# Attention in a four-layer network: products of values and probabilities in four column tiles, row sums on VectorE

## The chip, the cores and the metric

The kernel runs on one core of a Trainium2 chip. The metric is the time on the device in microseconds (us), as the median of several runs. Everything is computed in fp32.

## What is computed

The input x is a batch of B = 4 images with 384 channels and 64 x 64 positions. Four layers follow one another, each of the form x + layer(groupnorm(x)). The change lies in the first layer, whose core is single-head attention over the N = 4096 positions of an image:

```python
# layer 0, p = 96 of the 384 channels, per image
y   = layernorm_over_channels(groupnorm(x)[:, :96])
qkv = batchnorm(w_qkv @ y)               # 16 + 16 + 96 rows
q, k, v = qkv[:16], qkv[16:32], qkv[32:]
a   = softmax(q.T @ k * 0.25, axis=-1)   # 4096 x 4096
o   = v @ a.T                            # 96 x 4096
out = batchnorm(w_proj @ relu(concat([o, rest_of_channels])))
```

For each query position the 4096 exponentials are summed, and the weighted sum of the 96 value rows is divided by that sum. The second layer is a gated convolution layer with an 8 x 8 Fourier filter; layers three and four are convolutions and small products that the change does not touch.

## The kernel before, in words

The first phase, `phase_a`, covers layer 0 and most of layer 1. The attention of an image (`attention`) has 8 blocks `i` of 512 queries; each block has 8 steps `c` of 512 keys, so there are 64 steps an image and 256 in all. A step does the following.

- `scores` (line 715): four products with a contraction over 32 partitions, one for each of four groups `g` of 128 keys. They stand in four row tiles of the matrix array and fill a tile of four banks of PSUM (`sc_s`, one buffer).
- The exponentials (line 723): two ScalarE instructions of 128 x 1024 turn the scores into a tile `probs` of 128 keys by 4 x 512 (two buffers). The scores and exponentials of the next step are issued ahead of the products of this one, with raised priority.
- The products (line 752): four matmuls, each with all 128 keys of a group as the contraction, 128 columns of `vt` as the stationary operand, and 512 queries streaming. They add up over the 32 groups of a block in one PSUM bank `av` (tag "a", two buffers, so that successive blocks alternate).

`vt` has 128 columns: 96 value rows and 32 columns of ones, which the weight `wv` makes from the constant row of the normalised input. Rows 96 to 127 of `av` are thus 32 copies of the softmax sum. `finish` takes their reciprocal on VectorE (line 735) and scales and clips the 96 value rows in three instructions of 32 rows (line 738), since both operands lie 32 partitions wide. The result `xm` goes to the projection, `layer0_end` (lines 774 to 795), whose pieces are issued one a step during the next block.

What else runs beside the steps of image `b` is set by `side_by_side`: it takes pieces from `others`, which first reads the statistics of the next image (`x_norm`), then works through `layer1` of the image before, and makes `qkv` of the next image in between. Each piece carries a weight, and per step as many are issued as their even spread over 64 steps asks for. In `layer1` a tile of 16 columns goes through `t_m` (line 871), `coef_m` (886, emptied by VectorE at 888), `back_m` (896), and each band of eight rows through nine taps on VectorE for each of three channel blocks (line 948), which carry no weight, and then an output product `out_m` (965, 966; emptied by VectorE at 969). All these products, the projection's `proj_m` (785, emptied by VectorE at 792) and those of `qkv` share one PSUM tag, "m", with two buffers. PSUM has eight banks here: four for scores, two of tag "a", two of tag "m".

The order on each engine is fixed when the program is built: a scheduler keeps the order of issue as priority, lets an instruction go ahead where an earlier one isn't ready by its estimate, and puts in the semaphores. Every engine then works in that order.

Of the kernel before, what the change touches and what calls it, by code (L numbers as in the profile page):

```python
# [21 lines left out]
F32 = mybir.dt.float32  # L22
AF = mybir.ActivationFunctionType
ALU = mybir.AluOpType
# [5 lines left out]
P = 128  # L30
PD = 96
# [7 lines left out]
TAPS = (2, 2, 2, 2, 2, 2, 4, 4)  # L39

UNITS = C // 32

_CONST_COLS = {}
_VEC_COLS = {}
# [182 lines left out]
class _Builder:  # L227
    def __init__(self, ctx, tc, ins, out):
# [18 lines left out]

        self.tok = self.dram.tile([UNITS, B, 32, N], F32, tag="tok", name="tok")

# [137 lines left out]
    def qkv_weights(self, pool):  # L387

        nc = self.nc
        w = self.wk("wq_raw", "lx", 2)[:, 0:PD]
        nc.scalar.dma_start(w, self.ins["w_qkv"])
        inv, shift = self.bn_scale_shift(
            "bn1", self.vec("bn1_m"), self.vec("bn1_v"), self.vec("bn1_g"), self.vec("bn1_b")
        )
        nc.vector.tensor_scalar(w, w, inv, None, ALU.mult)
        pt = self.pm("wq_pt")
        nc.tensor.transpose(pt[0:PD, 0:P], w, self.ident)
        wt = self.wk("wq_t", "ln", 3)[0 : PD + 1, 0:P]  # L400
        raw = self.wk("wq_rawt", "lx", 2)[0:PD, 0:P]
        nc.vector.tensor_copy(raw, pt[0:PD, 0:P])
        nc.vector.tensor_scalar(wt[0:PD, :], raw, self.vec("ln_w", PD), None, ALU.mult)
        pb = self.pm("wq_pb")
        nc.tensor.matmul(pb[0:1, 0:P], lhsT=self.vec("ln_b", PD), rhs=raw, start=True, stop=False)
        nc.tensor.matmul(pb[0:1, 0:P], lhsT=shift, rhs=self.ident, start=False, stop=True)
        nc.scalar.copy(wt[PD : PD + 1, :], pb[0:1, 0:P])

        self.wq4 = pool.tile([PD + 1, 4, 32], F32, tag="wq4", name="wq4")
        self.wk4 = pool.tile([PD + 1, 4, 32], F32, tag="wk4", name="wk4")  # L410
        self.wv = pool.tile([PD + 1, P], F32, tag="wv", name="wv")
        for t in (self.wq4, self.wk4, self.wv):
            nc.gpsimd.memset(t, 0.0)
        nc.gpsimd.memset(self.wk4[PD : PD + 1, :, 0:1], 1.0)
        nc.gpsimd.memset(self.wv[PD : PD + 1, PD:], 1.0)
        for g in range(4):
            nc.vector.tensor_copy(self.wq4[:, g, 1:17], wt[:, 0:16])
            nc.vector.tensor_copy(self.wk4[:, g, 1:17], wt[:, 16:32])
        nc.vector.tensor_copy(self.wv[:, 0:PD], wt[:, 32:P])
        self.score_bound(pool, wt)  # L420

    def score_bound(self, pool, wt):
# [183 lines left out]
    def qkv_tiles(self):  # L606


        q = [None] * 8
        k4 = self.big.tile([P, 8, P], F32, tag="k4", name="k4", bufs=2)  # L610
        vt = self.big.tile([P, 32, P], F32, tag="vt", name="vt", bufs=2)
        return q, k4, vt

    def qkv(self, b, q, k4, vt):
        nc = self.nc

        xc, xn = [None] * 8, [None] * 8
        xc[0] = self.centered(b, 0)
        yield 1.0
        xn[0] = self.layer_norm(xc[0])  # L620
        xc[1] = self.centered(b, 1)
        yield 2.0
        for i in range(8):
            if i + 2 < 8:
                xc[i + 2] = self.centered(b, i + 2)
                yield 1.0
            if i + 1 < 8:
                xn[i + 1] = self.layer_norm(xc[i + 1])
                yield 1.0
# [12 lines left out]
            m = self.pm("v_m")  # L642
            mv = m.rearrange("p (c d) -> p c d", d=P)
            for c in range(4):
                nc.tensor.matmul(mv[:, c, :], lhsT=xa[:, c * P : (c + 1) * P], rhs=self.wv, start=True, stop=True)
            nc.vector.tensor_copy(vt[:, 4 * i : 4 * i + 4, :], mv)
            yield 2.8
# [55 lines left out]
    def attention(self, b, q, k4, vt):  # L703
# [3 lines left out]
        tc, nc = self.tc, self.nc  # L707
# [20 lines left out]
                )  # L728
            return p

        def finish(av):

            xm = self.work.tile([P, NJ, 512], F32, tag="xm", name="xm", bufs=1)
            rd = self.wk("av_rd", "rd", 1)
            nc.vector.reciprocal(rd[PD:P], av[PD:P])
            for g in range(3):
                at = slice(32 * g, 32 * g + 32)
                nc.vector.scalar_tensor_tensor(xm[at, 0], av[at], 0.0, rd[PD:P], ALU.max, ALU.mult)  # L738
            return xm

        st = self.stats_tile("xa_st")
        steps = [(i, c) for i in range(8) for c in range(8)]
        ahead = scores(*steps[0])
        done, end = None, iter(())
        for n_step, (i, c) in enumerate(steps):
            p = ahead
            if n_step + 1 < len(steps):
                ahead = scores(*steps[n_step + 1])
            if c == 0:
                av = self.pa("av")  # L750
            for v in range(4):
                nc.tensor.matmul(  # L752
                    av,
                    lhsT=vt[:, 4 * c + v, :],
                    rhs=p[:, v * 512 : (v + 1) * 512],
                    start=c == 0 and v == 0,
                    stop=c == 7 and v == 3,
                )
            next(end, None)
            if c == 1 and done is not None:  # L760
                end = self.layer0_end(b, i - 1, finish(done), st)
            if c == 7:
                done = av
            yield
        for _ in self.layer0_end(b, 7, finish(done), st):
            pass
        self.norm1 = self.norm_of_stats(st)

# [217 lines left out]
    def phase_b(self):  # L986
# [5 lines left out]
        with ExitStack() as ctx:  # L992
# [17 lines left out]
            self.units(cp)  # L1010
            self.unit_x = [[] for _ in range(UNITS)]
            for u in range(UNITS):
                st = self.bt_p.tile([P, 2, 16, 6], F32, tag="st", name="st")
                strips = self.unit_strips(u + 1) if u + 1 < UNITS else iter(())
                tok = self.unit_tok(u - 1) if u else self.unit_strips(0)
# [8 lines left out]
                self.conv_norms(u, st)  # L1024
            for _ in self.unit_tok(UNITS - 1):
                pass
# [859 lines left out]
```

## Time and profile before

| | |
|---|---|
| median of 3 runs | 4973.22 us (4967.2 to 4978.35) |
| span of the profiled execution | 4964.9 us |
| time around the span | not listed apart; the median lies 8.3 us above the span |
| TensorE busy | 4552.7 us (92%) |
| VectorE busy | 2769.8 us (56%) |
| ScalarE busy | 2136.4 us (43%) |
| attention: first to last product, line 752 | 81 to 2253 us of the span |

In a row of the page's slices each digit is the busy share of one fortieth of the span, in tenths. In a row of a group, the text after the line number names engine, operation, what is written from what, sizes and count; then come the busy time, the mean of one instruction in ns, and the idle time of the engine just before, with what ended it. A matmul of fp32 operands leaves two records in the profile, one for each of its two passes, and as many weight loads (PEld). Ends of matmuls are modelled; the distance from one start to the next is the better measure. In a row of the timeline the first two numbers are start and duration in us; neighbouring instructions of one line are merged.

### The profile page before, as it was taken

To read this page: it belongs to the slowest core of one execution; us is meant where nothing else is said; L and a number is where in the kernel's file an instruction comes from. 1 tells how busy PE (TensorE), PEld (TensorE's weight loads), DVE (VectorE), ACT (ScalarE), POOL (GpSimd) and SP (SyncE) were. 2 spreads that over 40 slices of the span, in tenths; PEclk is the share of its full clock that TensorE was granted. 3 is DMA by queue.
4 is the path that set the end of the run, shared out by engine and by line. 5 is a ranking of instruction groups with operands and counts; after the bars stand their busy time and mean duration, and the time that the engine had idled before them with its cause. 6 is when DMAs were issued, how large, how long until landed. Compare 5 with 4: busy or idle time off the path is not lost.

```text
span 4964.9 us, 47732 instructions
## 1 busy us (share of the span) xinstructions
PE 4552.7 (92%) x17665; PEld 2564.5 (52%) x17665; DVE 2769.8 (56%) x4438; ACT 2136.4 (43%) x2873; POOL 777.5 (16%) x593
## 2 busy tenths in 40 slices
PE   5999999999999999998989999699999998677988
PEld 2343444434443344444557888444444443577888
DVE  5322465644666445555867778655531112667898
ACT  4444344454444444444435666411123333764321
POOL 1000000000000000000025555100000001125554
PEclk9999999999999999998989999799999999699999
DMA  5210211211111111112338999776664443896776
GB/s 169 73 47 30 85 54 55 72 56 39 64 64 51 55 45 58 58 57 78 120 122 276 291 292 292 250 278 256 256 245 157 153 152 132 316 343 203 239 255 227
DMA packets 346710, 752.64 MB, mean 152 GB/s; under 512 B 22779, under 2 KB 173158, under 8 KB 337510
## 3 DMA queue, kind: packets, MB, share of 16 engines
q1 hardware_dynamic: 280728, 475.46, 30.1%
q0 software_dynamic: 32640, 151.28, 7.9%
q10 hardware_dynamic: 33102, 122.77, 6.3%
q8 instruction: 143, 2.34, 0.2%
q14 instruction: 97, 0.79, 0.0%
HBM read 447.16 MB, written 302.25 MB: 151 GB/s over the span
## 4 chain that ended last, share of the span: by engine, by line
PE 45%; DVE 9%; DMA 4%; ACT 3%; issue 3%; POOL 1%; SPq 0%; ACTq 0%; DVEq 0%; POOLq 0%
PE h_s L1380 10%; PE h_m L1432 10%; PE conv_m L1156 9%; PE av L752 3%; PE t_m L871 2%; PE conv_m L1757 2%; DVE acc L948 2%; DMA wmix<-in_mix_t 1%; DMA g_h<-h 1%; PE out_m L966 1%; PE proj_m L785 1%; PE sc_s L715 1%; DVE toep L1744 1%; PE taps_m L941 1%; DVE toep L1137 1%
## 5 line engine op out<-in xcount | busy, mean ns | idle before, releaser
L752 PE MATMUL av<-probs,vt 128*128 128x512 f32 x2048 | 965.6, 607 | 0.0
L723 ACT ACTIVATE probs<-sc_s 128x1024 f32<-128x1024 f32 x512 | 500.9, 1021 | 789.8 <-PE av L752 783.7
L752 PEld LDWEIGHTS av<-probs,vt 128*128 128x128 f32 x2048 | 371.7, 192 | 468.1 <-issue 461.0
L1156 PE MATMUL conv_m<-toep,z 128*128 128x256 f32 x2304 | 519.4, 385 | 10.6 <-DVE toep L1137 5.1
L948 DVE SCALAR_TENSOR_TENSOR acc<-band,vecs,acc 128x512 f32<-128x512 f32 x708 | 496.9, 747 | 45.7 <-POOL band L909 39.9
L1432 PE MATMUL h_m<-f_h,cm_w_t 128*128 128x512 f32 x1152 | 496.7, 595 | 8.7 <-ACT f_h L1422 8.7
L1156 PEld LDWEIGHTS conv_m<-toep,z 128*128 128x128 f32 x2304 | 439.4, 193 | 71.0 <-DVE z L1089 4.9
L1757 PE MATMUL conv_m<-toep,z 128*128 128x128 f32 x3072 | 392.8, 286 | 42.1 <-DVE toep L1744 19.2
L1757 PEld LDWEIGHTS conv_m<-toep,z 128*128 128x128 f32 x3072 | 378.7, 202 | 44.4 <-POOL toep L1744 18.2
L1380 PE MATMUL h_s<-e_tok,cm_w_t 128*128 128x512 f32 x768 | 363.4, 596 | 5.5 <-DVE e_tok L1365 5.5
L1137 POOL TENSOR_TENSOR toep<-w,band 128x1536 f32<-128x1536 f32 x94 | 324.0, 3447 | 278.0 <-PE conv_m L1156 232.0
L1432 PEld LDWEIGHTS h_m<-f_h,cm_w_t 128*128 128x128 f32 x1152 | 220.0, 191 | 285.4 <-issue 273.3
L715 PE MATMUL sc_s<-q,k 32*128 32x512 f32 x2048 | 296.3, 647 | 21.9 <-ACT probs L723 21.4
L1440 DVE BATCH_NORM_STATS2 h_st<-f_h 128x6 f32<-128x512 f32 x96 | 66.4, 694 | 429.1 <-ACT f_h L1439 429.1
L871 PE MATMUL t_m<-w_in_t,xb 128*128 128x384 f32 x768 | 276.7, 495 | 3.4 <-DVE coef L888 2.1
L1387 ACT COPY e_h<-h_s 128x1024 f32<-128x1024 f32 x96 | 97.2, 1012 | 401.5 <-PE h_s L1380 401.5
L785 PE MATMUL proj_m<-xm,w_proj_t 128*128 128x512 f32 x576 | 265.2, 599 | 4.6 <-DVE xm L738 3.5
L792 DVE SCALAR_TENSOR_TENSOR x_res<-proj_m,bn_c,x_res 128x512 f32<-128x512 f32 x96 | 71.8, 748 | 319.0 <-PE proj_m L785 315.9
L1380 PEld LDWEIGHTS h_s<-e_tok,cm_w_t 128*128 128x128 f32 x768 | 147.0, 192 | 189.5 <-issue 183.2
L1389 DVE BATCH_NORM_STATS2 h_st<-e_h 128x6 f32<-128x512 f32 x192 | 123.4, 685 | 202.8 <-ACT e_h L1387 202.8
L871 PEld LDWEIGHTS t_m<-w_in_t,xb 128*128 128x128 f32 x768 | 142.9, 192 | 139.0 <-issue 59.3
L1380 PE MATMUL h_s<-z,cm_w_t 128*128 128x512 f32 x384 | 196.2, 593 | 0.0
(380 smaller groups left out, 6206.2 us busy)
## 6 DMA issues: line engine op xcount, KB each, us to landing
d<-d_o ACTq DMA_DIRECT2D x96, 512.0 KB
c_d<-d SPq DMA_DIRECT2D x96, 512.0 KB
hid<-e_h ACTq DMA_DIRECT2D x16, 3072.0 KB
f_h<-hid SPq DMA_DIRECT2D x16, 3072.0 KB
x_in<-in_x SPq DMA_DIRECT2D x96, 256.0 KB
x_res<-in_x SPq DMA_DIRECT2D x32, 768.0 KB
xa<-x_res POOLq DMA_DIRECT2D x32, 768.0 KB, 3.9
xa_in<-xa SPq DMA_DIRECT2D x32, 768.0 KB
```

What stands on the lines that cost most here:

```text
L715: nc.tensor.matmul(s[:, g], lhsT=k4[32 * g : 32 * g + 32, c], rhs=q[i][32 * g : 32 * g + 32], start=True, stop=True,)
L723: nc.scalar.activation(p[:, h * 1024 : (h + 1) * 1024], s[:, 2 * h : 2 * h + 2].rearrange("p a b -> p (a b)"), AF.Exp, scale=0.25,)
L752: nc.tensor.matmul(av, lhsT=vt[:, 4 * c + v, :], rhs=p[:, v * 512 : (v + 1) * 512], start=c == 0 and v == 0, stop=c == 7 and v == 3,)
L785: nc.tensor.matmul(m, lhsT=self.w_proj[:, j, o * P : (o + 1) * P], rhs=xm[:, j], start=j == 0, stop=j == NJ - 1,)
L871: nc.tensor.matmul(m[:, 0:C], lhsT=xb[:, j], rhs=self.w_in[:, j, :], start=j == 0, stop=j == NJ - 1,)
L948: nc.vector.scalar_tensor_tensor(out, src(j, k), w, done, ALU.mult, ALU.add)
L1137: eng.tensor_tensor(t, self.w53[:, at : at + 192].rearrange("p (m n) -> p m n", n=8).unsqueeze(2).to_broadcast([P, 24, 8, 8]), band.rearra ...
L1156: nc.tensor.matmul(m[:, c * 256 : (c + 1) * 256], lhsT=self.z_[:, at : at + P], rhs=t[:, 12 * c + 4 * i : 12 * c + 4 * i + 4].rearrange("p ...
L1380: nc.tensor.matmul(s[:, v, :], lhsT=w1[:, j, o * P : (o + 1) * P], rhs=t[j][:, v * 512 : (v + 1) * 512], start=j == 0, stop=j == NJ - 1,)
L1389: nc.vector.bn_stats(st[:, o, 8 * b + 2 * i + v, :], h[:, o, v * 512 : (v + 1) * 512])
L1432: nc.tensor.matmul(m, lhsT=w2[:, o, j * P : (j + 1) * P], rhs=h[:, o, v * 512 : (v + 1) * 512], start=o == 0, stop=o == 5,)
L1757: nc.tensor.matmul(m[:, ch * P : (ch + 1) * P], lhsT=self.z_[:, at : at + P], rhs=t[:, 8 * c + 2 * i : 8 * c + 2 * i + 2].rearrange("p m a ...
```

## The change

The columns of ones go: `wv` and `vt` are 96 wide. The products of a step become twelve matmuls in place of four: for each of the four key groups `v`, the 96 value rows are taken as three slices `s` of 32. Each such matmul writes 32 partitions, one column tile `g` of the array. The table `PLAN` deals them out: three rounds of four, in which each column tile has one matmul. As twelve jobs of three slices don't divide into four tiles by slice, there are two banks, `av[0]` and `av[1]`, both of tag "a"; slice 0 is summed in tiles 0 and 3 of the first bank, slice 1 in tile 1 of the first and tile 0 of the second, slice 2 in tile 2 of the first and tile 1 of the second.

The softmax sums are made apart. In each step VectorE adds the two halves of `probs` (128 x 1024 each) to an accumulator `acc_p` in SBUF; the first step of a block makes it from one addition. After the last step one addition of 128 x 512 leaves `sum_p`. In `finish`, one product with a 128 x 96 matrix of ones sums it over partitions and spreads it to 96 rows.

At the end of a block `evacuate` copies the two banks to SBUF: 96 rows and 32 rows by VectorE, twice 32 rows by ScalarE. `finish` then adds both parts, takes the reciprocal over 96 rows and scales and clips 96 rows in one instruction.

```diff
+PLAN = (
+    ((0, 0, 3), (0, 1, 2), (0, 2, 1), (0, 0, 0)),
+    ((1, 1, 0), (0, 1, 3), (0, 2, 2), (0, 0, 1)),
+    ((1, 1, 1), (1, 2, 0), (0, 2, 3), (0, 0, 2)),
+)
...
-        self.wv = pool.tile([PD + 1, P], F32, tag="wv", name="wv")
+        self.wv = pool.tile([PD + 1, PD], F32, tag="wv", name="wv")
+        self.ones = pool.tile([P, PD], F32, tag="ones", name="ones")
+        nc.gpsimd.memset(self.ones, 1.0)
...
-        nc.gpsimd.memset(self.wv[PD : PD + 1, PD:], 1.0)
...
-        vt = self.big.tile([P, 32, P], F32, tag="vt", name="vt", bufs=2)
+        vt = self.big.tile([P, 32, PD], F32, tag="vt", name="vt", bufs=2)
...
-            mv = m.rearrange("p (c d) -> p c d", d=P)
+            mv = m[:, 0 : 4 * PD].rearrange("p (c d) -> p c d", d=PD)
...
-        def finish(av):
+        def products(av, c, p):
+
+            quarter = lambda g: slice(32 * g, 32 * g + 32)
+            for n, jobs in enumerate(PLAN):
+                for g, (k, s, v) in enumerate(jobs):
+                    others = [x[g] for x in PLAN[:n]], [x[g] for x in PLAN[n + 1 :]]
+                    before, behind = (any(x[:2] == (k, s) for x in o) for o in others)
+                    nc.tensor.matmul(
+                        av[k][quarter(g)],
+                        lhsT=vt[:, 4 * c + v, quarter(s)],
+                        rhs=p[:, v * 512 : (v + 1) * 512],
+                        start=c == 0 and not before,
+                        stop=c == 7 and not behind,
+                    )
+
+        def add_up(c, p):
+
+            lo, hi = p[:, 0:1024], p[:, 1024:2048]
+            if c == 0:
+                self.acc = self.probs.tile([P, 1024], F32, tag="acc", name="acc_p", bufs=1)
+                nc.vector.tensor_add(self.acc, lo, hi)
+            else:
+                nc.vector.tensor_add(self.acc, self.acc, lo)
+                nc.vector.tensor_add(self.acc, self.acc, hi)
+            if c == 7:
+                self.prob_sum = self.probs.tile([P, 512], F32, tag="sum", name="sum_p", bufs=1)
+                nc.vector.tensor_add(self.prob_sum, self.acc[:, 0:512], self.acc[:, 512:1024])
+
+        def evacuate(av):
+
+            a, t = self.wk("av_a", "rd", 1), self.wk("av_t", "av_t", 1)
+            nc.scalar.copy(t[0:32], av[0][96:128])
+            nc.vector.tensor_copy(a[0:PD], av[0][0:PD])
+            nc.scalar.copy(t[32:64], av[1][0:32])
+            nc.vector.tensor_copy(t[64:96], av[1][32:64])
+            return a, t, self.prob_sum
+
+        def finish(a, t, total):
 
             xm = self.work.tile([P, NJ, 512], F32, tag="xm", name="xm", bufs=1)
-            rd = self.wk("av_rd", "rd", 1)
-            nc.vector.reciprocal(rd[PD:P], av[PD:P])
-            for g in range(3):
-                at = slice(32 * g, 32 * g + 32)
-                nc.vector.scalar_tensor_tensor(xm[at, 0], av[at], 0.0, rd[PD:P], ALU.max, ALU.mult)
+            m = self.pm("sum_m")
+            nc.tensor.matmul(m[0:PD], lhsT=self.ones, rhs=total, start=True, stop=True)
+            nc.vector.tensor_add(t[0:PD], t[0:PD], a[0:PD])
+            nc.vector.reciprocal(a[0:PD], m[0:PD])
+            nc.vector.scalar_tensor_tensor(xm[0:PD, 0], t[0:PD], 0.0, a[0:PD], ALU.max, ALU.mult)
             return xm
...
-                av = self.pa("av")
-            for v in range(4):
-                nc.tensor.matmul(
...
-                )
+                av = self.pa("av_0"), self.pa("av_1")
+            products(av, c, p)
+            add_up(c, p)
+            if c == 7:
+                evacuated = evacuate(av)
             next(end, None)
             if c == 1 and done is not None:
-                end = self.layer0_end(b, i - 1, finish(done), st)
+                end = self.layer0_end(b, i - 1, finish(*done), st)
             if c == 7:
-                done = av
+                done = evacuated
```

More of the change, by code (lines that the diff above doesn't have):

```diff
@@ L418, in qkv_weights @@
             nc.vector.tensor_copy(self.wk4[:, g, 1:17], wt[:, 16:32])
-        nc.vector.tensor_copy(self.wv[:, 0:PD], wt[:, 32:P])
+        nc.vector.tensor_copy(self.wv, wt[:, 32:P])
         self.score_bound(pool, wt)
@@ L749, in attention @@
             if c == 0:
-                av = self.pa("av")
-            for v in range(4):
[L752 to L757, printed above, removed]
-                )
+                av = self.pa("av_0"), self.pa("av_1")
[3 more added lines that the diff above has]
+                evacuated = evacuate(av)
             next(end, None)
             if c == 1 and done is not None:
-                end = self.layer0_end(b, i - 1, finish(done), st)
+                end = self.layer0_end(b, i - 1, finish(*done), st)
             if c == 7:
-                done = av
+                done = evacuated
             yield
-        for _ in self.layer0_end(b, 7, finish(done), st):
+        for _ in self.layer0_end(b, 7, finish(*done), st):
             pass
```

## The prediction

> **What bounds the kernel now.** I read the page's slices first. They place the change: the products of the attention, line 752, run from 81 to 2253 us of the span, the first 18 of 40 slices.
>
> ```profile
> PE   5999999999999999998989999699999998677988
> DVE  5322465644666445555867778655531112667898
> ...
> L752 PE MATMUL av<-probs,vt 128*128 128x512 f32 x2048 | 965.6, 607 | 0.0
> L723 ACT ACTIVATE probs<-sc_s 128x1024 f32<-128x1024 f32 x512 | 500.9, 1021 | 789.8 <-PE av L752 783.7
> ```
>
> TensorE stands at 9 there and never sat idle ahead of a product; ScalarE's exponentials waited 784 us for it. VectorE has room, but unevenly. The busy time of each engine by stage sharpens this (columns after the window: its length, then PE, PEld, DVE, ACT, POOL, granted clock, DMA):
>
> ```profile
> 81.00:560.00 479.00, 448.56 (x1467) 182.12 (x1466) 158.31 (x248) 212.29 (x238) 11.93 (x20) 0.99 0.18 58
> 600.00:1000.00 400.00, 394.01 (x1312) 173.50 (x1311) 245.98 (x392) 187.60 (x233) 18.67 (x37) 1.00 0.17 59
> 1200.00:1600.00 400.00, 391.43 (x1297) 171.31 (x1298) 250.06 (x395) 189.43 (x234) 13.96 (x29) 0.99 0.17 57
> 1800.00:2253.00 453.00, 446.56 (x1455) 191.32 (x1454) 258.89 (x405) 202.94 (x246) 14.82 (x29) 1.00 0.17 57
> 81.00:2253.00 2172.00, 2098.49 (x6962) 906.04 (x6961) 1098.21 (x1828) 1001.56 (x1199) 75.05 (x141) 0.99 0.18 58
> ```
>
> Image 0 (first row) leaves VectorE at 33%. Beside the convolution layer of the image before, it is at 57 to 63%. The timeline of all engines gives the pace inside one step:
>
> ```profile
> 303.92 1.14 PE L715 MATMUL sc_s<-q,k 32*128 32x512 f32 x8
> 304.99 3.70 PE L752 MATMUL av<-probs,vt 128*128 128x512 f32 x8
> 308.53 2.74 PE L785 MATMUL proj_m<-xm,w_proj_t 128*128 128x512 f32 x6
> ```
>
> Four products are eight records, two passes each, for these fp32 operands. They take 304.99 to 308.53, 3.54 us. Weight loads within the group lie 0.43 us apart, so eight passes make 3.43 and the first load 0.11. The scores, four row tiles side by side, need 1.07 us for eight passes of the same length: two rounds (0.86) and 0.21 for a change of tiling. That 0.21 is the price of each border between tilings.
>
> The timeline of VectorE shows a burst:
>
> ```profile
> 1432.22 9.20 DVE L948 SCALAR_TENSOR_TENSOR acc<-band,vecs,acc 128x512 f32<-128x512 f32 x13
> 1441.33 0.85 DVE L863 TENSOR_SCALAR xb<-xa_in,gn_gm,gn_r 128x128 f32<-128x128 f32 x3
> 1442.10 0.55 DVE L888 TENSOR_TENSOR coef<-filt,coef_m 128x384 f32<-128x384 f32 x1
> ```
>
> Thirteen taps in a row hold up a coefficient product whose matmul TensorE had finished by about 1438.1. Such stretches without a pause, 18.7 to 28.4 us long, occur 24 times between 600 and 2250 us, one for each band of eight rows of images 0 to 2; together about 580 us, 24 us each.
>
> **The Trainium skill.** "TensorE: Matmul & The Clock Gate", in the part on packing small matmuls, gives 3.07x for four row tiles and 2.38x for three column tiles. The trace agrees on rows (3.43/1.07 = 3.2x); it holds no column tiles side by side. "TensorEngine Tiling (Array Packing)", Key Properties, says "Mode switching requires drain"; the trace's 0.21 us a border is its size. "VectorE: DVE Perf Modes", in the perf-mode tier table, keeps fp32 tensor_tensor at one element a cycle; the trace has
>
> ```profile
> L1744 DVE TENSOR_TENSOR toep<-wmix,band_p 128x1024 f32<-128x1024 f32 x129 | 155.4, 1212 | 27.1 <-DMA wmix<-in_mix_t 16.6 <-PE conv_m L1757 8.6 <-issue 1.5
> ```
>
> **The change, part by part.** There are 4 images x 8 blocks x 8 steps = 256 steps and 32 blocks.
>
> TensorE, products: 12 of 128x32 in place of 4 of 128x128. Side by side in four column tiles they are 3 rounds of two passes, 6 x 0.429 = 2.57 us for 3.43: -0.858 x 256 = -220 us. Bounds: no gain of overlap gives 24 x 0.429 = 10.3 us a step (+1760); the skill's 2.38 of 3 (79% of ideal) gives 3.25 us (-46). I take the full overlap, since the row tiles of this trace keep it over both rounds.
>
> TensorE, borders: products now differ in tiling from projection and convolution too. Counted from the timeline, the products stand in 358 uninterrupted groups, so 716 borders, of which 201 touch scores and were paid already. If the groups stay, 515 are new; if each step's products stay in one, about 370. I take 450 x 0.21 = +95.
>
> TensorE, rest: one product of 128x96 by 512 a block, two passes: 32 x 0.86 = +27. The value matmuls stream 96 columns for 128: 256 passes x 0.027 = -7. Sum for TensorE: -220 + 95 + 27 - 7 = **-105 us**.
>
> VectorE, sums: a block has 1 + 7 x 2 additions of 128x1024 at 1.212 us (18.2) and one of 128x512 at 0.69: 18.9. Evacuation and finish: two PSUM copies (0.69 each, as L646) and one addition (0.69) come in; the reciprocal (3.36) keeps its 512 columns; three scaled maxima (0.684 each) become one: +0.70. The value copy is 384 wide for 512: -0.14. That is 19.4 a block, **+622 us** on VectorE, 2.43 a step.
>
> Is that hidden? Image 0 has 64 steps in its row: 158 + 156 = 314 of 479 - 26 = 453 us: yes, behind the products. From 600 to 1000 there are 46 steps: 246 + 112 = 358 of 400 - 46 x 0.41 (105/256) = 381, 94%; from 1200 to 1600, 95%; from 1800 on, 92%. On average VectorE still fits, but within a burst it doesn't: three steps add 7 us to 24, while TensorE would pass the same steps 1 us sooner. VectorE falls 8 us behind.
>
> Who waits for that? The new additions read the probabilities, of which there are two buffers, so the exponentials of the step after next wait for them; behind those stand the next scores, as the score buffer is single. This loop has slack: probabilities made from 1409.5 to 1411.5 are used from 1419.8 on. But the coefficient, projection and output matmuls share two PSUM buffers that VectorE empties, with hardly any slack (the row at 1442.10). Neither is in the trace of before at this load, so I bound it: 0 us a burst if the order of work shifts around it, 8 us if all reaches TensorE; I take 4.5: 24 x 4.5 = **+108**.
>
> Accumulators: both banks of tag "a" are now one block's, where they alternated. The first products of a block wait for two VectorE and two ScalarE copies, which stand behind the last additions on VectorE. From last product to free bank: two copies, 1.4 us, and two hand-overs of 0.1 (an exponential that waits for products ending at 1443.57 starts at 1443.67), 1.6 in all. A score group (1.07) and other layers' work lie in between. Bounds 0 to 32 x 1.6 = 51 (more only if a burst is ahead, counted above); I take 0.8: **+26**. ScalarE gains 64 copies of about 0.57 us, 37 us on an engine at 46%, in front of an exponential that waits for the same products: nothing. The memset of ones and the narrower weight come before the first scores: nothing. No DMA moves, none is added, and SP's and POOL's queues keep theirs.
>
> Sum: -105 + 108 + 26 = +29. The span is 4964.9 us; the execution's time around it isn't given, so I take the median's distance, 8.3 us, as what lies around. 4964.9 + 29 + 8.3 = 5002, say **5003 us**. (The three runs shown are 4967.2 to 4978.4.)
>
> **The rivals.**
> *The bursts are absorbed; faster.* Decision point: a lag reaching TensorE of (105 - 26)/24 = 3.3 us a burst. For it: 14 us from the end of one exponential pair (1411.5) to the end of the products that use it (1425.4), and a nearly idle VectorE after each burst (5 us of work from 1442.7 to 1462). At 0.5 us a burst: -105 + 12 + 26 = -67, **4906 us**. Against it: the 94% and the shared PSUM buffers.
> *Columns overlap less than rows.* At the skill's 79%, the products save 46, not 220: -46 + 95 + 27 - 7 = +69, and with VectorE less pressed (half the lag) +54 + 26: **5122 us**. With no overlap at all, some 6700. For it: column tiles all read the same partitions, and the trace has none. Against it: the skill's measured three.
> *VectorE becomes the bound outright.* All 8 us a burst, and 51 for the accumulators: -105 + 192 + 51 = +138, **5111 us**. The long tap bursts run ahead of additions issued later, which speaks for it.
>
> **How the numbers follow.** Forecast (4.5 us a burst, 3 to 7) 36%, of which 3 end faster and 4 near zero; absorbed 36%, of which 6 end near zero; VectorE outright 18%; columns poorer 10%. 0.2% is 10 us, about what a measurement here tells from no change. Faster 0.30 + 0.03 = 0.33, within 0.2% 0.10, slower 0.29 + 0.18 + 0.10 = 0.57. The range runs from the absorbed case with a quarter of the borders unpaid, 4880, to above both slow cases, 5150; serial columns stay outside. The likeliest slow cases alone give 4985 to 5110.
>
> **What would show it.** Right: product groups of 24 records in about 2.8 us; 480 additions of 128x1024 at 1.21 us; VectorE near 1720 us over the attention; exponentials and scores newly waiting for VectorE's sums; TensorE idle in the burst stretches, not in image 0, which ends earlier by about 20 us. Wrong: groups of 24 records well above 3 us (columns), or TensorE still at 97% beside bursts of 31 us (absorbed). The stages after the attention should not change.

## The result, and the profile after

| | before | after |
|---|---|---|
| median | 4974.24 us | 5014.94 us (5013.58 to 5018.17) |
| ratio to before | 1 | 1.0082, 95% interval 1.0069 to 1.0095 |
| span of the profiled execution | 4964.9 us | 5016.4 us |
| TensorE busy | 4552.7 us | 4549.3 us |
| VectorE busy | 2769.8 us | 3337.1 us |

The change makes the kernel slower, by 41 us of the medians; the forecast was 5003. (The profiled execution of after was the slowest of its four, 5018.17 us, so its span lies above the median.) The total is close. The sum behind it is not: the products' gain was 84 us smaller than forecast, and borders and waits together cost 79 us less.

The page of after, slices and groups (in a group: busy time, mean ns of one, then the idle time ahead of it with its cause):

```profile
PE   5899899999999999998989999699999998677988
...
DVE  5666688776788668885877778655531112677898
...
L746 PE MATMUL av<-probs,vt 128*32 128x512 f32 x6144 | 836.1, 614 | 16.9 <-DVE av_t L773 14.6
L731 ACT ACTIVATE probs<-sc_s 128x1024 f32<-128x1024 f32 x512 | 499.3, 1021 | 639.6 <-PE av L746 634.7
...
L761 DVE TENSOR_TENSOR acc_p<-acc_p,probs 128x1024 f32<-128x1024 f32 x224 | 272.6, 1217 | 181.9 <-ACT probs L731 180.5
```

The products are three times as many instructions and together only a little shorter (836 us for 966). The exponentials wait for products, as before, 635 us. An addition costs what the forecast took from the Toeplitz row. Its idle time says who is late: VectorE waits for the exponential, not the other way round. Stage by stage (length, then PE, PEld, DVE, ACT, POOL, granted clock, DMA):

```profile
87.50:560.00 472.50, 435.52 (x2559) 135.72 (x2558) 304.90 (x386) 220.65 (x252) 11.93 (x20) 0.95 0.18 57
600.00:1000.00 400.00, 373.63 (x1972) 135.98 (x1972) 328.52 (x468) 166.31 (x216) 20.52 (x34) 0.99 0.18 61
1200.00:1600.00 400.00, 381.25 (x2022) 140.97 (x2025) 325.39 (x464) 171.40 (x223) 12.64 (x26) 0.99 0.16 54
1800.00:2291.00 491.00, 469.33 (x2555) 165.81 (x2556) 396.00 (x542) 211.06 (x268) 15.15 (x30) 0.99 0.16 53
87.50:2291.50 2204.00, 2075.18 (x11116) 729.97 (x11116) 1653.51 (x2359) 996.32 (x1228) 78.22 (x141) 0.97 0.17 57
```

VectorE stands at 81 to 82% where 92 to 95% were forecast. The stage is longer (the second row holds 43 steps, where the forecast had 46), and neighbouring instructions of VectorE overlap by about 0.1 us in the profile, so busy time grows by less than the durations that the forecast added. TensorE fell from 97% of the attention to 94%: it now pauses. That is 2204 us from first to last product for 2172.

The timeline of TensorE shows what happened to the products:

```profile
1443.32 1.05 PE L746 MATMUL av<-probs,vt 128*32 128x512 f32 x2
1444.30 1.14 PE L723 MATMUL sc_s<-q,k 32*128 32x512 f32 x8
1445.68 0.94 PE L937 MATMUL back_m<-to_pos,coef 128*128 128x128 f32 x6 [0.25 <-DVE coef L929]
1446.55 2.78 PE L746 MATMUL av<-probs,vt 128*32 128x512 f32 x22
1449.26 2.20 PE L912 MATMUL t_m<-w_in_t,xb 128*128 128x384 f32 x6
```

The group of 22 records runs as hoped: in it, starts come in fours 7 ns apart, and the fours are 0.43 us apart. The four column tiles overlap fully. But the scheduler put the first of the twelve products ahead of the scores, alone. It takes two passes (0.98 us to the next start) in one column tile with three tiles idle. The eleven that are left still need three products of two passes in the fullest tile, six rounds (2.71 us). Nothing is saved by having done one beforehand; the step has paid for eight rounds. In all, 126 of the 256 steps were split: 55 into one product and eleven, 35 into nine and three, 23 into five and seven, the rest otherwise. The kernel before was split in the same way at no loss, because each of its products fills the array.

I counted this over the attention. Records that start within 35 ns of one another in different tiles are a round; a pass of 512 columns lasts 0.427 us. A border into row tiles or the whole array takes 0.21 us: in the median about 0.10 ahead of its first pass and 0.106 between that and the second. A border into column tiles takes 0.125: 0.10 and 0.026. What is left of the distance to the next start is a wait. So the sum closes by construction, and an error in the price of a border would stand in the waits.

| from first to last product, us | forecast | counted |
|---|---|---|
| products | -220 | -136 (1728 rounds; unbroken groups need 1536) |
| borders between tilings | +95 | +66 (635 to 1094, 459 more; 352 lead into column tiles) |
| `sum_m` / narrower `v_m` | +27 / -7 | +26.5 / -6.4 |
| waits: bursts 108, accumulators 26 | +134 | +84 (147 to 231) |
| other instructions | 0 | -2 |
| sum | +29 | +32 |

The extra 192 rounds are 82 us. Outside this stretch the first products come 6 us later (why, no run tells; the granted clock of the 100 us from there on is 0.84, where it was 0.98), and the last block's projection ends 47 us later where the last product is 38 later: after the last product, the sums, copies, `sum_m` and the reciprocal stand in a row between the last taps, with no product of a next block to hide them.

```profile
2296.34 0.69 DVE L765 TENSOR_TENSOR sum_p<-acc_p 128x512 f32<-128x512 f32 x1
2296.94 0.75 DVE L989 SCALAR_TENSOR_TENSOR acc<-band,vecs,acc 128x512 f32<-128x512 f32 x1
2297.60 0.68 DVE L771 COPY av_a<-av 96x512 f32<-96x512 f32 x1
...
2307.70 2.02 PE L780 MATMUL sum_m<-sum_p,ones 128*96 128x512 f32 x2
...
2309.75 3.35 DVE L782 RECIPROCAL av_a<-sum_m 96x512 f32<-96x512 f32 x1 [0.54 <-PE sum_m L780]
2313.14 0.69 DVE L783 SCALAR_TENSOR_TENSOR xm<-av_t,av_a 96x512 f32<-96x512 f32 x1
2313.98 9.52 PE L826 MATMUL proj_m<-xm,w_proj_t 128*128 128x512 f32 x18 [4.26 <-DVE xm L783]
```

From the last product (2291.5) to the projection 22 us pass; before, it was 13 (2253.5 to 2266.8). This tail of 9 us was not in the forecast. The stages behind it keep this distance to within 7 us, as forecast.

### The profile page after: what moved, and what is told of

It is laid out like the page before. It is cut to its first block, busy times and chain, and to the rows that moved or that the text cites. A ratio compares the mean times of both kernels' runs of the same rounds, so it can differ in the third digit from the quotient of the medians.

```text
span 5016.4 us, 56968 instructions
## 1 busy us (share of the span) xinstructions
PE 4549.3 (91%) x21825; PEld 2400.9 (48%) x21825; DVE 3337.1 (67%) x4982; ACT 2136.3 (43%) x2909; POOL 780.5 (16%) x593
## 4 chain that ended last, share of the span: by engine, by line
PE 62%; DVE 18%; ACT 6%; issue 6%; DMA 5%; POOL 1%; SPq 0%; ACTq 0%; POOLq 0%; DVEq 0%
PE h_s L1421 10%; PE h_m L1473 10%; PE av L746 10%; PE conv_m L1197 9%; DVE acc L989 5%; PE sc_s L723 3%; PE proj_m L826 3%; PE t_m L912 2%; PE conv_m L1798 2%; PE out_m L1007 2%; PE out_m L1006 1%; PE back_m L937 1%; DVE acc_p L761 1%; ACT probs L731 1%; DMA wmix<-in_mix_t 1%
## 5 line engine op out<-in xcount | busy, mean ns | idle before, releaser
L746 PE MATMUL av<-probs,vt 128*32 128x512 f32 x6144 | 836.1, 614 | 16.9 <-DVE av_t L773 14.6
L746 PEld LDWEIGHTS av<-probs,vt 128*32 128x32 f32 x6144 | 186.4, 111 | 511.8 <-issue 457.1
L761 DVE TENSOR_TENSOR acc_p<-acc_p,probs 128x1024 f32<-128x1024 f32 x224 | 272.6, 1217 | 181.9 <-ACT probs L731 180.5
L762 DVE TENSOR_TENSOR acc_p<-acc_p,probs 128x1024 f32<-128x1024 f32 x224 | 273.0, 1219 | 15.7 <-ACT probs L731 6.1
```

What stands on the lines that cost most here:

```text
L746: nc.tensor.matmul(av[k][quarter(g)], lhsT=vt[:, 4 * c + v, quarter(s)], rhs=p[:, v * 512 : (v + 1) * 512], start=c == 0 and not before, s ...
L761: nc.vector.tensor_add(self.acc, self.acc, lo)
```

## Experiments: which half of the change costs what

The traces name two causes, broken groups with their borders on TensorE and waits that VectorE's sums bring. The first four kernels take each half alone or undo it. Kernels that were run at different times are compared "by the ratios": the difference of their ratios to before, times the 4970 us of before.

**Whole groups.** Each product is issued behind the one ahead of it, the scores behind the last product, and the group with raised priority.

```diff
-                    nc.tensor.matmul(
+                    with ExitStack() as order:
+                        if n or g:
+                            order.enter_context(tc.high_priority())
+                        if self.last_pe is not None:
+                            order.enter_context(tc.issue_after(self.last_pe.ins))
+                        self.last_pe = nc.tensor.matmul(
...
-            with tc.high_priority():
+            with ExitStack() as order:
+                order.enter_context(tc.high_priority())
+                if self.last_pe is not None:
+                    order.enter_context(tc.issue_after(self.last_pe.ins))
                 for g in range(4):
-                    nc.tensor.matmul(
+                    self.last_pe = nc.tensor.matmul(
                         s[:, g],
...
```

> The changed kernel with the order of TensorE alone constrained: the twelve products of a step stay together and alternate with the scores. The work on every engine is that of the changed kernel (5015 us). Theory A, that of the prediction (VectorE's bursts take back about 108 us of what TensorE gains): the order on TensorE is hardly the matter, and fewer borders give 5015 - 30 to 50 = about 4970, with TensorE's waits grown in place of what was saved. Theory B (broken groups): 193 rounds with one column tile alone cost 193 x 0.429 = 83 us, and some 240 borders of 0.21 go too, 50 us: 5015 - 133 = about 4885, and still below 4920 if a third of it comes back as waits.

Measured: 4944.9 us, ratio 0.9945 (0.9928 to 0.9961). The change with its groups whole is faster than the kernel before. From first to last product the span falls by 70 us, to 2133.7: rounds of products 1728 to 1553 (-75), borders 1094 to 874 (-38), waits 231 to 249 (+18). The scores in turn are broken more often, 568 rounds for 510 (+25). Its timeline, and a row of its waits (us in total, times, longest):

```profile
1449.10 0.91 PE L936 MATMUL coef_m<-t_t,to_coef 128*128 128x384 f32 x2 [1.97 <-DVE x_res L842]
1449.94 2.78 PE L754 MATMUL av<-probs,vt 128*32 128x512 f32 x24
...
PE coef_m L936 <- DVE x_res L842: 35.0, 15, 4.4
```

All 24 records stand together in 2.78 us. The new wait is that of a coefficient product for a tag-m buffer, which the projection's result holds until VectorE has taken it.

**Sums left out.** `add_up` is not called; `sum_m` reads a constant tile.

```diff
+        self.flat = pool.tile([P, 512], F32, tag="flat", name="flat")
+        nc.gpsimd.memset(self.flat, 1.0)
...
-            return a, t, self.prob_sum
+            return a, t, self.flat
...
-            add_up(c, p)
```

> The changed kernel without the additions of the probabilities on VectorE; the product that spreads the sums reads a constant tile instead, so the softmax sums are left out. Everything else is as changed. Theory A: the 108 us that VectorE's bursts cost go, about 4905. Theory B: the groups stay broken; only the part of the 54 us of added waits that is VectorE's goes, 20 to 50 us: 4965 to 4995.

Measured: 4965.64 us, 0.9986 (0.9979 to 0.9993), 48 us under after by the ratios. The waits fall from 231 to 189 us; rounds and borders stay (1716 and 1100). So the additions, 606 us of VectorE's time by their own durations, cost TensorE 42 us of waits. As many, 189 for 147 in before, are new without any addition.

**Sums alone.** The products as before, on the whole array and with one bank a block, with the columns of ones gone; sums on VectorE as in after.

```diff
         def products(av, c, p):
...
+            for v in range(4):
+                nc.tensor.matmul(
+                    av[0:PD],
+                    lhsT=vt[:, 4 * c + v, :],
+                    rhs=p[:, v * 512 : (v + 1) * 512],
...
-                av = self.pa("av_0"), self.pa("av_1")
+                av = self.pa("av")
             products(av, c, p)
             add_up(c, p)
...
```

> Half of the change alone: sums on VectorE and spread by one product a block, value rows 96 wide, but products on the whole array (four of 128x96 a step into one alternating bank), with no column tiles, no second bank and no evacuation. Theory A: the kernel before (4974) + 108 for the bursts + 27 for the spreading product - 7 = about 5100. Theory B: waits of 20 to 40 us + 20 = 5015 to 5035.

Measured: 5043.16 us, 1.0147 (1.013 to 1.0164). The waits rise by 50 us over before (147 to 197), and `sum_m` adds its 26. Two comparisons with quite different products thus agree: the sums cost 42 to 50 us of waits, not 108. The column tiles, on the other hand, do bring something even broken: after is 32 us faster than this kernel.

**Before, with whole groups.** The order constraint of whole groups, put on the four products of before; the scores are tied as there (not shown).

```diff
+                with ExitStack() as order:
+                    if v:
+                        order.enter_context(tc.high_priority())
+                    order.enter_context(tc.issue_after(self.last_pe.ins))
-                nc.tensor.matmul(
+                    self.last_pe = nc.tensor.matmul(
                         av,
...
```

> The kernel before, with the same constraint on TensorE's order: the four products of a step stay together and alternate with the scores. Broken groups cost nothing there, as products share their tiling with projection and convolution, so both theories expect only fewer borders with the scores and perhaps a wait more: 4974 within 25 us. If it gains much more than that, the gain of the whole groups in the changed kernel is not due to column tiles.

Measured: 5009.47 us, 1.0073 (1.0056 to 1.0089). Its products gain nothing from standing together, its scores are broken more often (550 rounds for 511, +17 us), and its waits rise by 29 us (147 to 177). The constraint has a price of its own, 46 us in waits and scores, about the 43 us that whole groups shows of them; that kernel won in spite of it.

## Experiments: where VectorE's work is waited for

**Sums a step later.** `add_up` of a step is issued ahead of the next step's products, not behind its own.

```diff
+            if n_step:
+                add_up(*behind)
-            p = ahead
+            p, behind = ahead, (c, ahead)
...
-            add_up(c, p)
...
+        add_up(*behind)
```

> The changed kernel with the additions of a step issued one step later in the program, behind that step's pieces of other work. In the changed kernel VectorE stands 213 us at the head of its queue for exponentials that its next addition needs. Theory A (the bursts hold up the sums, and the sums the exponentials): the sums now stand behind one more step's taps, exponentials wait for them, slower than 5015 by 20 us or more. Theory C (the additions are too early in VectorE's queue, and projection, coefficient and output products queue behind them): 10 to 35 us faster, 4980 to 5005, and VectorE's wait for exponentials falls under 80 us.

Measured: 5025.2 us, 1.0111 (1.0096 to 1.0126). Issuing them later brings nothing; the loss against after is 14 us by the ratios, of intervals that nearly touch, and 4 us of the attention in the profiles. At `acc_p` VectorE still waits 187 us for exponentials, where theory C set under 80. Theory C fails; A has the sign, but not the size.

**The sum taken out of PSUM first.** ScalarE copies `sum_m`, so that its tag-m buffer is free before the reciprocal of 3.35 us.

```diff
-            nc.vector.reciprocal(a[0:PD], m[0:PD])
+            nc.scalar.copy(a[0:PD], m[0:PD])
+            nc.vector.reciprocal(a[0:PD], a[0:PD])
```

> The changed kernel with the spread sums first copied from their PSUM buffer of tag m to SBUF by ScalarE (0.57 us), and the reciprocal of 3.35 us then taken there. Theory D: the sums hold one of the two buffers of tag m until the reciprocal ends, and the waits of coef_m, out_m and gn_pg for it, 51 us in TensorE's queues counted with weight loads, are about half real: 15 to 30 us faster, 4985 to 5000. Rival: VectorE is behind anyway, the next product waits for the next instruction of VectorE instead, and the time stays within 8 us of 5015.

Measured: 5006.11 us, 1.0069 (1.0055 to 1.0082). In after this wait looks as follows (timeline, then two rows of the waits: us in total, times, longest):

```profile
1241.22 0.91 PE L912 MATMUL t_m<-w_in_t,xb 128*128 128x384 f32 x2
1244.50 0.91 PE L927 MATMUL coef_m<-t_t,to_coef 128*128 128x384 f32 x2 [2.36 <-DVE av_a L782]
1245.25 1.40 PE L937 MATMUL back_m<-to_pos,coef 128*128 128x128 f32 x6
1246.57 3.84 PE L746 MATMUL av<-probs,vt 128*32 128x512 f32 x24
...
PE coef_m L927 <- DVE av_a L782: 17.7, 9, 3.1
PE back_m L937 <- ACT t_t L920: 24.7, 14, 2.6
```

A coefficient product waits 2.36 us for the buffer that the reciprocal holds, and the 24 records behind it take 3.84 us, not 2.78: the granted clock stands at half from 1245.3 to 1248.8. The wait for the reciprocal happens nine times in after (17.7 us) and not at all here, and coefficient products behind `t_m` wait 4 us in all, in place of 22. But `back_m` still waits 23 us for ScalarE's copy of `t_m`, and the waits in and behind the attention's products rise from 37 to 51. In the one profile the attention is 17 us shorter, in the runs 6 us of the two ratios, whose intervals overlap: a small gain at best.

**Banks emptied by one engine each.** VectorE takes both parts of bank 0, ScalarE both of bank 1.

```diff
-            nc.scalar.copy(t[0:32], av[0][96:128])
             nc.vector.tensor_copy(a[0:PD], av[0][0:PD])
+            nc.vector.tensor_copy(t[0:32], av[0][96:128])
             nc.scalar.copy(t[32:64], av[1][0:32])
-            nc.vector.tensor_copy(t[64:96], av[1][32:64])
+            nc.scalar.copy(t[64:96], av[1][32:64])
```

> The changed kernel with each accumulator bank emptied by one engine: bank 0 by two VectorE copies, bank 1 by two ScalarE copies, where before both engines took turns in both banks. In the changed kernel VectorE's last copy waits 51 us in all for ScalarE's copy of the other quarter of its bank, and the next block's products then wait for it (49 us in TensorE's queues). Theory E: about half of that goes, 10 to 25 us faster, 4990 to 5005. Rival (the banks' hand-over is covered by other products): within 8 us of 5015.

Measured: 5007.33 us, 1.0067 (1.0054 to 1.008). In after VectorE's copy waited 51.5 us, in 18 blocks, for ScalarE's copy of the same bank, which is itself late; here that wait is gone. TensorE's own wait for the accumulators goes from 16 to 11 us. Of the ratios it is 7 us; the intervals overlap, so this too is a small gain at best.

**Whole groups, scores free.** The products are chained among themselves, the scores are not tied to them. Against whole groups:

```diff
-            with ExitStack() as order:
-                order.enter_context(tc.high_priority())
-                if self.last_pe is not None:
-                    order.enter_context(tc.issue_after(self.last_pe.ins))
+            with tc.high_priority(1000):
                 for g in range(4):
-                    self.last_pe = nc.tensor.matmul(
+                    nc.tensor.matmul(
...
-                        if self.last_pe is not None:
                             order.enter_context(tc.issue_after(self.last_pe.ins))
...
```

> Whole groups again, by priority alone: a step's products 2 to 12 follow the first at top priority, scores keep a smaller advance (1000 instructions), and nothing ties scores to products. Theory B (broken groups are the loss) with the tying of scores as the 40 us that the same constraint cost the kernel before: below the 4945 of whole_groups by 10 to 40 us, 4905 to 4935. Rival: what costs is that other layers' products are pushed behind whole groups of 2.7 us, with two buffers of tag m: the same 4945 within 10 us.

Measured: 4950.3 us, 0.995 (0.9938 to 0.9963), the same as with tied scores. There are fewer broken score groups (540 rounds for 568) and more borders (947 for 874): what one gives, the other takes.

## Experiments: a better version, and what bounds it

**Whole groups with both repairs.** Three of the diffs above together: whole groups, the sum taken out, a bank to an engine.

> The kernel after with whole groups (12 products of a step in a row), with ScalarE taking sum_m out of PSUM ahead of the reciprocal, and with bank 0 of the accumulators emptied by VectorE and bank 1 by ScalarE. Theory A (three separate costs): the 70 us of whole groups and the 8 or 9 us of each of the other two add up: 4928 us, and beyond-stream time of TensorE some 17 us under the 227 of whole groups alone. Rival B (the pressure only moves: what one wait gives back, VectorE's queue takes at the next one): 4940 to 4950, no better than whole groups alone (4945).

Measured: 4937.53 us, 0.9936 (0.992 to 0.9953), the fastest kernel here that makes the sums, below before and after. Against whole groups alone it is 4 us by the ratios, well inside the intervals; the rival's 4940 to 4950 is nearer than theory A's 4928, so that the repairs add up is not shown. Coefficient products still wait 42 us for `x_res`.

**Whole groups without sums.** Two of the diffs above together: whole groups, sums left out.

> The kernel after with whole groups, its additions on VectorE left out (sum_m reads a constant tile, so the softmax sums are not those of the reference). It sizes the sums where the groups are whole. Theory A (VectorE's additions cost the more, the denser TensorE's work is; coef_m and others newly wait some 80 us for x_res and further VectorE work): 4865 to 4885 us, 60 to 80 under whole groups. Rival B (the waits of whole groups are those of work pushed behind the groups, as the same order cost the kernel before 38 us): 4905 to 4925, the 20 to 40 that the sums cost without whole groups, or less.

Measured: 4906.33 us, 0.9875 (0.9854 to 0.9895), 35 us under whole groups. The sums cost no more where TensorE is denser; theory A's 60 to 80 fails.

**Part of the additions on GpSimd.** To whole groups with both repairs this adds, from step 2 of a block on:

```diff
...
-                nc.vector.tensor_add(self.acc, self.acc, hi)
+                nc.gpsimd.tensor_add(self.prob_sum, self.prob_sum, hi[:, 0:512])
+                nc.gpsimd.tensor_add(self.prob_sum, self.prob_sum, hi[:, 512:1024])
...
```

> As whole_both, but from step 2 of a block on GpSimd adds the second half of probs to an accumulator of its own (two additions of 128x512 a step), VectorE only the first half; at the end two additions of 128x512 join them. VectorE loses some 192 additions of 1.21 us (-230 us), GpSimd gains 352 additions, estimated at 1.15 us each from its 128x1536 multiplication of 3.45 us (+400 us). Theory A (VectorE's load is what costs): 20 to 35 us under whole_both. Rival B (GpSimd's additions hold probs longer or make VectorE's own instructions longer): no gain, or slower than whole_both; then VectorE's additions of 128x1024 last longer than 1.22 us, or exponentials wait for GpSimd.

Measured: 5038.41 us, 1.0135 (1.0115 to 1.0155), 99 us slower than whole groups with both repairs, though VectorE's busy time on the page falls from 3336 to 3254 us. The groups of the attention in this kernel:

```profile
L777 POOL TENSOR_TENSOR sum_p<-sum_p,probs 128x512 f32<-128x512 f32 x160 | 243.8, 1523 | 552.0 <-ACT probs L734 535.8 <-ACT gn_r L322 13.0
...
L776 DVE TENSOR_TENSOR acc_p<-acc_p,probs 128x1024 f32<-128x1024 f32 x160 | 211.7, 1323 | 199.9 <-ACT probs L734 199.8
...
L1007 DVE SCALAR_TENSOR_TENSOR acc<-band,vecs,acc 128x512 f32<-128x512 f32 x708 | 543.6, 810 | 27.6 <-POOL band L968 19.4 <-ACT acc L1005 3.5
...
L851 DVE SCALAR_TENSOR_TENSOR x_res<-proj_m,bn_c,x_res 128x512 f32<-128x512 f32 x96 | 71.6, 746 | 44.6 <-PE proj_m L844 44.3
```

and the same taps with both repairs but no work on GpSimd:

```profile
L999 DVE SCALAR_TENSOR_TENSOR acc<-band,vecs,acc 128x512 f32<-128x512 f32 x708 | 499.1, 745 | 25.2 <-POOL band L960 19.7 <-ACT acc L997 0.6
```

The taps lasted 810 ns in place of 745, the additions 1323 in place of 1219, while `x_res`, of the same shape but with one operand in PSUM, stayed at 746 (743). Exponentials waited for GpSimd as well, 14 times, 37 us together. TensorE's waits rose by 113 us; about 40 of these lie between first and last tap of the bursts, and some 70 if the 6 us behind each last tap are counted. Both effects of the rival are there; how the 99 us divide between them was not separated.

**Tag-m buffers freed first.** To whole groups with both repairs this adds raised priority for `x_res`, `coef` and `xa_out`; the three edits are alike.

```diff
...
+        with self.tc.high_priority():
             nc.vector.tensor_mul(cf, self.filt, m[:, 0:C])
...
```

> As whole_both, but the three VectorE instructions that free a tag-m buffer (x_res behind proj_m, coef behind coef_m, xa_out behind out_m) are issued with raised priority, ahead of additions and taps where the scheduler sees them ready. Theory A (tag-m buffers wait in VectorE's queue behind additions): the waits of coef_m for x_res shrink, 15 to 30 us under whole_both. Rival B (the scheduler's estimate already puts them as early as they can go, or the additions put off in turn hold probs): within 8 us of whole_both.

Measured: 4946.35 us, 0.9951 (0.9932 to 0.9969): no gain over 0.9936. Coefficient products wait 43 us for `x_res` as before. Raised priority does not bring `x_res` forward: in both kernels it starts 0.82 us behind the end of its product in the median. What lies between the projection and its removal is left open.

## Why the prediction came out near

That the total came near is luck: one term was 84 us too favourable, and others were too dear by about as much.

**Products, -220: the step that failed.** The overlap of the column tiles was right: 22 records from 1446.55 on in 2.71 us, and with whole groups 24 in no more than 2.78, with no trace of the 2.38 of 3 for column tiles in the Trainium skill ("TensorE: Matmul & The Clock Gate", Part 3). The term was mis-sized because it assumed that every group stays whole: "3 rounds of two passes" holds only if the twelve stand together. In its paragraph on borders the forecast had itself counted 358 groups for 256 steps, and asked what the extra groups cost in borders, not what they cost in rounds. It measured -136. The whole-groups kernel shows the difference on the clock: 68 us by the ratios.

**Borders, +95: oversized.** The count was right, 459 new ones for 450 forecast. The price, 0.21 us, was read at borders of the scores and holds there; a border into column tiles takes 0.125, and the new ones come to +66. So the 0.21 is not the size of every change of tiling.

**Bursts, +108: oversized.** The mechanism was a VectorE that falls 8 us behind within a burst. The direction is shown: from the first tap on, TensorE's waits are 26 us longer in after than without the sums, and 50 us longer in the kernel with sums alone than in before. In the tap stretches, counted to some 6 us behind the last tap, they rise by 28 and 42 us; up to the last tap alone by 36 and 20 (the stretches are also longer with additions between the taps). How much of it is the bursts is thus open for the second pair. If all of the rise from the first tap on is put down to the 24 bursts it is 1.1 to 2.1 us each for the 4.5 taken. Ahead of the first tap, the sums alone cost nothing, and after 17 us more than without its sums, of which 8.6 are one stall at 173 us, where products waited for VectorE's copy of the accumulators. Why so little? The forecast set the additions behind a finished burst. The order that was built puts them between the taps (timeline of VectorE in after):

```profile
1404.78 2.08 DVE L989 SCALAR_TENSOR_TENSOR acc<-band,vecs,acc 128x512 f32<-128x512 f32 x3
1406.77 1.23 DVE L761 TENSOR_TENSOR acc_p<-acc_p,probs 128x1024 f32<-128x1024 f32 x1
1407.90 0.75 DVE L989 SCALAR_TENSOR_TENSOR acc<-band,vecs,acc 128x512 f32<-128x512 f32 x1
1408.56 0.75 DVE L833 SCALAR_TENSOR_TENSOR x_res<-proj_m,bn_c,x_res 128x512 f32<-128x512 f32 x1
1409.23 1.22 DVE L762 TENSOR_TENSOR acc_p<-acc_p,probs 128x1024 f32<-128x1024 f32 x1
```

The taps can be late; the additions seldom are. That this order is the reason is read from it, not tested: no run sets the additions behind whole bursts. A step's additions end 2.4 us behind its exponentials in the median (6.9 at the ninth decile, 23.1 at most), and in every step before the exponential that needs the buffer, by 11.4 us in the median and never less than 0.37.

**"Exponentials newly waiting for VectorE's sums": wrong.** They don't wait for them at all in after; in the kernel with sums alone, once, for 5.4 us. The forecast's remark that this loop has slack was right and should have carried the point. The waits fell, as it said, on the tag-m buffers.

**Accumulators, +26.** The wait for `av_t` and `av_a` is there, 16 us, inside its bounds (0 to 51) and somewhat over half the value taken; without the sums it is 4. Giving a bank to one engine saves 7 us at most.

**"Image 0 ends earlier by about 20 us".** From its first exponential to the next image's it is 453 us for 460, a gain of 7. With whole groups it is 419. In after 43 of its 64 steps were split, and it has no bursts; what each of the two is worth was not separated.

**VectorE, +622.** Summed over the durations of its changed instructions it came to +623. Busy time, in which overlaps count once, rose by 567 us, and over the attention it is 1653.5 us, not 1720.

**Missed.** Half of the 84 us of new waits, 42, come without the additions (147 to 189 us in the kernel without sums). `sum_m` takes one of the two tag-m buffers and holds it through a reciprocal of 3.35 us. The wait of `coef_m` for it is 17.7 us (13.9 without the sums), and more at the clock. `back_m` waits 24.7 us for ScalarE's copy of `t_m`, where it was 5.5 in before and is 14.8 without the sums. The rest was not separated. The last block's tail is 9 us.

**The rivals.** "The bursts are absorbed" had its turning point at 3.3 us a burst; the measured 1.1 to 2.1 lies below it. By the forecast's own sum the kernel should then have been faster, and with whole groups it is. So the sign came out right by luck, through the broken groups, which no case named. "Columns overlap less" is excluded by these 2.71 us. "VectorE becomes the bound" is excluded by 81% and by the slack above.

## What to carry to other kernels

Where several small products share the array, the gain belongs to the round, not to the product: look in the trace for how often the scheduler already splits such a group, and price a split in rounds, not only in borders. An engine that rises from 57 to 82% does not cost what its queue would suggest, if, as here it seems, the new work is ready early and can be put between work that may be late; ask which instruction of the queue has a waiter. A sum that comes out right has to be checked term by term, since errors of some 80 us can hide each other.

## What the hardware showed that was not expected

**A pause can cost twice.** The Trainium skill, "TensorE: Matmul & The Clock Gate", Part 1, says that TensorE falls to half its clock after an idle window of about 3.4 us. Here it did so after shorter pauses: of the 21 stretches of after's attention in which the granted clock stands at half, and passes take 0.85 us in place of 0.43, 19 begin in a pause of over 1 us or within 14 us behind it. Not every pause does it: of 47 pauses of over 1 us, 21 were followed by half clock within 7 us, of the 15 of 2.5 us or more 11. The two stretches of the timeline in this text show both outcomes (ahead of 1244.50 a wait of 2.36 us, and then 24 records in 3.84 us; ahead of 1445.68 one of 0.25, and then the full pace). Counted on passes of 512 columns or near it alone, the slow ones cost 22 us in after, 8 in before, 10 without the sums and 39 with whole groups: by this count 14 of the 84 us of new waits are the clock.

**Four column tiles keep the full pace.** Passes in four tiles start 7 ns apart and the next four 0.43 us later, though the two passes of one fp32 product follow one another in its own tile.

**GpSimd slows some of VectorE's instructions.** The Trainium skill, "GPSIMD Engine Reference", Key points, says that it contends with VectorE's instructions that have two inputs in SBUF or run in a two-port mode. The trace agrees, instruction by instruction: taps that overlap a GpSimd addition for more than half their time last 1253 ns in the mean, those that meet none 744; additions 1477 and 1217. The one-input instruction that makes `xb` lasts 979 for 339; no run tells its mode. Those with an operand in PSUM don't change (`x_res` 749 and 743), nor does the reciprocal (3342).
